# LSTM steps as 2x2 block products in Strassen's seven-product form, in a four-layer graph network

## The chip, the cores and the metric

The kernel runs on one core of a Trainium2 chip. Times are device microseconds of one execution, from its launch to its end, and the figure compared is the median of several. The core has five engines that work side by side and wait for each other through semaphores: TensorE (PE) multiplies matrices and writes to eight banks of accumulation memory (PSUM, 512 fp32 columns each), VectorE (DVE) and ScalarE (ACT) do element-wise work and read those banks, GpSimd (POOL) does element-wise work on the main on-chip memory (SBUF), and SyncE (SP) issues transfers. All data are fp32.

## The reference

The input x is (128, 64, 256): 128 graphs of 64 nodes with 256 features, and one 64x64 adjacency matrix. Each of four layers adds to x the result of a graph layer on `relu(layernorm(x))`:

```python
# layer 0: two graph convolutions, then four LSTMs over windows of p = 1..4 nodes
h = relu(adj @ (x @ Wg0 + bg0)); h = relu(adj @ (h @ Wg1 + bg1))
for p in range(1, 5):
    nw = 64 // p
    wins = h[:, :nw*p, :].reshape(B*nw, p, 256)
    # LSTM over the p nodes of a window; g = x_t @ Wih[p-1].T + h @ Whh[p-1].T + b
    # c = sigmoid(f)*c + sigmoid(i)*tanh(g);  h = sigmoid(o)*tanh(c)
    h = h.at[:, arange(nw)*p + p-1, :].set(last hidden state)
# layer 1: normalised adjacency, linear 256->512, batch norm, relu, linear 512->256, batch norm
# layer 2: three products with W[k], combined by diagonal, upper and lower part of adj
# layer 3: one attention head, qkv = x @ Wqkv, causal softmax(q k^T / 16 + adj) v, @ Wo
```

The first LSTM step of a window has no h term, as h starts at zero.

## The kernel before, in words

Rows are the 8192 nodes, in 16 pieces of 512 (`NS`) or 4 groups of 2048 (`NG`). Stages follow one another:

1. `graph_part` (lines 229 to 259): layer norm and the two graph convolutions, piece by piece, written to `hT`, which holds features in partitions (two halves `c`) and nodes along the free axis, one tile per group.
2. Lines 269 to 285: `wqkv` and `wo` are loaded and the products `wqk` and `wvo` of layer 3's weights are made (12 transposes and 8 products), before the LSTMs.
3. The LSTMs, for p = 1 to 4. The windows of a group are cut into blocks of at most 512 columns (16 windows of 32 graphs): N is 512 for p = 1, 2 and 4, and 320 or 352 for p = 3. `step` does one time step of one block: for each gate in the order i, g, f, o and each half of its 256 outputs, two products with `wih` and, from the second step on, two with `whh` into one bank (line 329), then one activation by ScalarE (line 331). VectorE makes the cell (338, 341 to 343), ScalarE its tanh (344), VectorE h (347) or the result in `hT` (351). Two blocks alternate, so that one's cell work lies beside the other's products. A scheduler orders the instructions there.
4. `first_product` (layer 1 up to its first linear layer, with `hs` copies by GpSimd at 395), batch norm 1, `second_product`, batch norm 2 (`bn_coeffs`).
5. `rest`: layers 2 and 3, piece by piece.

Within `pipelined` stages, as in any `manual_schedule` block, each engine's queue has its instructions in the order in which the code writes them. `psum` has eight one-bank buffers taken in turn by `bank()`. Pools on the left of SBUF (`hpool`, `lg`, `lh`, `pz`, `pb`, `wt`, `pc`) and on the right (`hlast`, `lw`, `first`, `late`) are stacked; a tile of a later pool waits for the last use of what lay in its place. The loads of `wih` and `whh` are issued by SP, most constants by ScalarE's queue.

Of the kernel before, what the change touches and what calls it, by code (L numbers as in the profile page):

```python
# [14 lines left out]
P = 128  # L15
# [5 lines left out]
def kernel(ctx: ExitStack, tc: tile.TileContext, a: dict, out: bass.AP):  # L21
# [40 lines left out]
    lstm_weights, lw = other_end("lw", 2)  # L62
# [22 lines left out]
    ones = const.tile([P, P], F32, tag="ones", name="ones")  # L85
# [4 lines left out]
    def block_diag(name, src):  # L90
        t = const.tile([P, P], F32, tag=name, name=name)
        nc.vector.memset(t, 0.0)
        for r in range(0, P, T):
            nc.scalar.dma_start(t[r : r + T, r : r + T], src)
        return t
# [9 lines left out]
    w1 = weight("w1", a["W1T"])  # L105
    w2 = weight("w2", a["W2T"])
    bn1 = load_const("bn1", a["bn1"], [P, 3, HC])
    bn2 = load_const("bn2", a["bn2"], [P, 3, KC])
    wqk = const.tile([P, KC, D], F32, tag="wqk", name="wqk")
    wvo = const.tile([P, KC, D], F32, tag="wvo", name="wvo")  # L110
# [79 lines left out]
    def to_token_major(src, add, dst):  # L190

        for q2 in range(0, Q, 2):
# [8 lines left out]
    hbuf = [(hpool if g < NG else hlast).tile([P, KC, GRP], F32, tag=f"hT{g}", name=f"hT{g}")  # L201
            for g in range(NG + 1)]
    hT = hbuf[1:]
# [63 lines left out]
    with tc.tile_pool(name="wt", bufs=1) as wt:  # L267
        wqkv = wt.tile([P, KC, 3 * D], F32, tag="wqkv", name="wqkv")
        nc.scalar.dma_start(wqkv, a["Wqkv"].rearrange("(c p) m -> p c m", p=P))
        wo = wt.tile([P, KC, D], F32, tag="wo", name="wo")  # L270
        nc.scalar.dma_start(wo, a["Wo"].rearrange("(c p) m -> p c m", p=P))
        wT = wt.tile([P, 3 * KC, D], F32, tag="wT", name="wT")
        for k in range(3):
            p_ = bank().rearrange("p (d c) -> p d c", d=KC)
            for d in range(KC):
                for c in range(KC):
                    nc.tensor.transpose(p_[:, d, ts(c, P)], wqkv[:, c, ts(k * KC + d, P)], ident)
            nc.vector.tensor_copy(wT[:, k * KC : (k + 1) * KC, :], p_)
        for left, right, to in ((0, wT[:, KC : 2 * KC, :], wqk), (2, wo, wvo)):
            p_ = bank().rearrange("p (c m) -> p c m", c=KC)  # L280
            for c in range(KC):
                for d in range(KC):
                    nc.tensor.matmul(p_[:, c, :], wT[:, left * KC + d, ts(c, P)], right[:, d, :],
                                     start=(d == 0), stop=(d == KC - 1))
            nc.vector.tensor_copy(to, p_)


    with tc.tile_pool(name="lg", bufs=2) as lg, \
            tc.tile_pool(name="lh", bufs=3) as lh:
        for p in range(1, NL + 1):  # L290
            l = p - 1
            wih = lw.tile([P, KC, G4], F32, tag="wih", name="wih")
            nc.sync.dma_start(wih, a["WihT"][l].rearrange("(c p) m -> p c m", p=P))
            whh = None
            if p > 1:
                whh = lw.tile([P, KC, G4], F32, tag="whh", name="whh")
                nc.sync.dma_start(whh, a["WhhT"][l].rearrange("(c p) m -> p c m", p=P))
# [4 lines left out]
            blocks = [(g, w0, w1 - w0) for g in range(NG) for w0, w1 in zip(cut, cut[1:])]  # L302
# [6 lines left out]
            def step(blk, j, state):  # L309
                last = j == p - 1  # L310
                N = blk[2] * GB
                gate = {}
                for name, gi, fn in (("i", 0, AF.Sigmoid), ("g", 2, AF.Tanh),
                                     ("f", 1, AF.Sigmoid), ("o", 3, AF.Sigmoid)):
                    if name == "f" and j == 0:
                        continue
# [39 lines left out]
            for k in range(0, len(blocks), 2):  # L356
                pair = [(blk, {}) for blk in blocks[k : k + 2]]
                for j in range(p):
                    for blk, state in pair:
                        step(blk, j, state)  # L360
# [228 lines left out]
```

## Time and profile before

| | us |
|---|---|
| median of three executions (2129.55 to 2130.78) | 2130.47 |
| the profiled execution | 2128.89 |
| its span, first to last instruction | 2127.2 |
| TensorE busy in the span | 2064.4 (97%) |
| VectorE, ScalarE, GpSimd busy | 788.5, 739.0, 139.0 |
| graph part: until the last matmul of line 252 | 0 to 189.0 |
| LSTMs: first to last matmul of line 329 | 202.4 to 1384.0 |
| first product and batch norm 1 | 1384 to 1569 |
| second product and batch norm 2 | 1569 to 1685 |
| rest | 1685 to 2127 |

Engines are busy side by side, so their sums pass the span. The ends of matmuls are modelled by the profiler, so a group's mean can be longer than the distance from one matmul to the next; that distance is read from the timeline. In the groups of instructions a row has line, engine and operation, the tiles written and read, shapes and count, then busy microseconds and mean nanoseconds of one, then the idle time of the engine ahead of them and who ended it.

### The profile page before, as it was taken

The page shows a single profiled execution, that of the slowest core. Times are in us where ns is not written, and L with a number is a line of the kernel's source. Part 1 is how long each engine was busy: PE and PEld are TensorE (multiplying, and loading weights), DVE is VectorE, ACT ScalarE, POOL GpSimd, SP SyncE. Part 2 cuts the span into 40 slices and gives each one's busy share as a digit, 9 for nine tenths or more (in the row PEclk, how much of TensorE's full clock was granted, in tenths as well). Part 3 has the DMA queues.
Part 4 walks back from the last instruction along what each step waited for, and adds up shares of the span by engine and source line. Part 5 has one row for each costly group of instructions (what it writes and reads, how often), then busy time and mean ns, then how long its engine had stood idle before and what let it go on. Part 6 is the DMA issues. An engine that isn't in the chain of part 4 may idle for free. (4 is left out here: it accounts for less than half of the span.)

```text
span 2127.2 us, 18649 instructions
## 1 busy us (share of the span) xinstructions
PE 2064.4 (97%) x7488; PEld 1241.0 (58%) x7488; DVE 788.5 (37%) x1569; ACT 739.0 (35%) x1267; POOL 139.0 (7%) x126
## 2 busy tenths in 40 slices
PE   6998999999999999999999999989999799999998
PEld 5775444444445666666444444455544478888887
DVE  5773222112121122121211211177744455555553
ACT  3553444332233233232322322234463033333332
POOL 1000000000000000000000000032200021111110
PEclk9999999999999999999999999999999899999999
DMA  5100000000001000000000000033300000111111
GB/s 193 50 30 20 0 0 20 0 0 0 0 0 40 1 0 1 0 1 0 0 0 0 0 0 0 0 121 97 107 10 0 30 20 20 41 40 41 44 47 40
DMA packets 35975, 54.26 MB, mean 26 GB/s; under 512 B 2608, under 2 KB 29488, under 8 KB 35888
## 3 DMA queue, kind: packets, MB, share of 16 engines
q1 hardware_dynamic: 31856, 49.29, 7.1%
q10 hardware_dynamic: 4032, 3.78, 0.6%
q8 instruction: 59, 0.97, 0.2%
q14 instruction: 28, 0.23, 0.0%
HBM read 36.28 MB, written 16.78 MB: 25 GB/s over the span
## 5 line engine op out<-in xcount | busy, mean ns | idle before, releaser
L329 PE MATMUL ps<-hT,wih 128*128 128x512 f32 (+2 forms) x2016 | 808.9, 541 | 0.0
L329 PEld LDWEIGHTS ps<-hT,wih 128*128 128x128 f32 x2016 | 383.0, 190 | 378.5 <-issue 313.3
L329 PE MATMUL ps<-hn,whh 128*128 128x512 f32 (+2 forms) x1152 | 466.3, 527 | 0.0
L329 PEld LDWEIGHTS ps<-hn,whh 128*128 128x128 f32 x1152 | 218.9, 190 | 200.4 <-issue 153.1
L176 ACT ACTIVATE ln_h<-x,ln_rn 128x256 f32<-128x256 f32 x192 | 99.6, 589 | 368.1 <-DVE ln_rn L173 363.2
L341 DVE TENSOR_TENSOR gi<-gi,gg 128x1024 f32<-128x1024 f32 (+2 forms) x36 | 38.2, 1062 | 385.6 <-ACT gg L331 385.6
L331 ACT ACTIVATE gi<-ps,lbias 128x512 f32<-128x512 f32 (+2 forms) x144 | 91.9, 638 | 235.0 <-PE ps L329 235.0
L331 ACT ACTIVATE gg<-ps,lbias 128x512 f32<-128x512 f32 (+2 forms) x144 | 91.9, 638 | 232.0 <-PE ps L329 232.0
L485 PE MATMUL ps<-wl,ag 128*128 128x256 f32 x768 | 169.6, 381 | 0.0
L485 PEld LDWEIGHTS ps<-wl,ag 128*128 128x128 f32 x768 | 145.7, 191 | 19.3
L331 ACT ACTIVATE go<-ps,lbias 128x512 f32<-128x512 f32 (+2 forms) x144 | 91.2, 634 | 89.2 <-PE ps L329 86.8
L338 DVE TENSOR_TENSOR cell<-gi,gg 128x1024 f32<-128x1024 f32 (+2 forms) x36 | 41.1, 1143 | 201.2 <-ACT gg L331 201.2
L395 POOL COPY hs<-hT 128x512 f32<-128x512 f32 x32 | 33.5, 1078 | 1228.9 <-PE ps L329 1228.9
L407 PE MATMUL ps<-ag,w 128*128 128x512 f32 x256 | 112.3, 592 | 0.0
L331 ACT ACTIVATE gf<-ps,lbias 128x512 f32<-128x512 f32 (+2 forms) x72 | 44.8, 622 | 164.9 <-PE ps L329 164.9
L342 DVE TENSOR_TENSOR cell<-gf,cell 128x1024 f32<-128x1024 f32 (+2 forms) x36 | 38.2, 1062 | 171.4 <-ACT gf L331 171.4
L172 POOL TENSOR_TENSOR ln_rn<-ln_rn,mhalf 128x4 f32<-128x4 f32 x64 | 64.6, 1010 | 537.1 <-DVE ln_rn L171 537.1
L344 ACT ACTIVATE gg<-cell 128x1024 f32<-128x1024 f32 (+1 forms) x72 | 68.7, 954 | 82.2 <-DVE cell L343 82.2
L351 DVE TENSOR_TENSOR hT<-go,gg 128x512 f32<-128x512 f32 (+2 forms) x72 | 47.1, 654 | 86.6 <-ACT go L331 62.4
L407 PEld LDWEIGHTS ps<-ag,w 128*128 128x128 f32 x256 | 47.5, 190 | 54.0 <-issue 50.7
L169 DVE BATCH_NORM_STATS2 ln_st<-x 128x6 f32<-128x256 f32 x192 | 76.9, 401 | 0.0
L347 DVE TENSOR_TENSOR hn<-go,gg 128x1024 f32<-128x1024 f32 (+2 forms) x36 | 38.2, 1062 | 94.9 <-ACT go L331 94.9
(127 smaller groups left out, 1965.7 us busy)
## 6 DMA issues: line engine op xcount, KB each, us to landing
xt<-in_x_dram SPq DMA_DIRECT2D x32, 512.0 KB, 4.5
x1d<-x SPq DMA_DIRECT2D x16, 512.0 KB, 2.9
x<-x1d SPq DMA_DIRECT2D x16, 512.0 KB, 4.6
out_dram<-x SPq DMA_DIRECT2D x16, 512.0 KB, 3.2
wih<-in_WihT_dram SPq DMA_DIRECT2D x4, 1024.0 KB, 6.2
whh<-in_WhhT_dram SPq DMA_DIRECT2D x3, 1024.0 KB, 7.8
wqkv<-in_Wqkv_dram ACTq DMA_DIRECT2D x1, 768.0 KB, 4.3
wl<-in_W_dram ACTq DMA_DIRECT2D x3, 256.0 KB, 3.1
```

The costliest lines, as they stand in the source:

```text
L169: nc.vector.bn_stats(st[:, q, :], src[:, q, :])
L172: nc.gpsimd.tensor_tensor(rn[:, 0, :], rn[:, 0, :], mhalf[:, :Q], ALU.pow)
L176: nc.scalar.activation(h[:, q, :], src[:, q, :], AF.Relu, bias=rn[:, 1, q : q + 1], scale=rn[:, 0, q : q + 1])
L329: nc.tensor.matmul(o_, w[:, c, ts(m, P)], r, start=(n == 0), stop=(n == len(ops) - 1))
L331: nc.scalar.activation(gt[:, hc, :N], p_[:, :N], fn, bias=lbias[:, l, m : m + 1])
L338: nc.vector.tensor_mul(c_, i_, g_)
L341: nc.vector.tensor_mul(i_, i_, g_)
L342: nc.vector.tensor_mul(c_, gate["f"][:, :, :N], c_)
L344: nc.scalar.activation(g_, c_, AF.Tanh)
L351: nc.vector.tensor_mul(cols(blk, c, j), gate["o"][:, c, :N].rearrange("p (w b) -> p w b", b=GB), gate["g"][:, c, :N].rearrange("p (w b) -> ...
L407: nc.tensor.matmul(p_, w1[:, c, ts(o, P)], ag[:, c, :], start=(c == 0), stop=(c == KC - 1))
L485: nc.tensor.matmul(p_[:, q, :], ag[:, c, k, ts(q2 + q, P)], wl2[k][:, c, :], start=(n == 0), stop=(n == 3 * KC - 1))
```

## The change

Two blocks of columns are now taken together as a 2x2 problem: the rows of the left factor are the two halves of a gate's 256 outputs, the inner blocks the two halves of the features, and the columns the two blocks of windows. From the second step on (`strassen`) each gate is made of seven block products in place of eight, each with one `wih` and one `whh` matmul. The factors are sums and differences: of weights, made by GpSimd (`weight_sums`) after each load; of the inputs, by VectorE (`input_sums`); of h, by VectorE after each step. The outputs are put together from three copies out of the accumulating bank by ScalarE and three additions by VectorE per gate, and four activations follow, three of them from SBUF. The first step of a window (`plain`) keeps its products. The cell's element-wise work moves from VectorE to GpSimd. Two gates are in work at a time (`staggered`), and the whole LSTM part is written in a `manual_schedule`.

The products of layer 3's weights move behind batch norm 2, with the copies by ScalarE in place of VectorE, and their loads ahead of `second_product`. `lw` has one buffer (with two for `wih`), `w1` and `w2` are loaded behind the LSTMs, the adjacency blocks and `ones` lie in `first`, and the spare group tile `hS` is made behind the LSTMs.

In the compiled program a stretch of the Strassen steps has, with A the older gate and B the younger, this order of products on TensorE: A7, B1, A4, B2, A3, B6, B5, then B7, C1, B4 and so on; the numbers are those of `product`. ScalarE's queue has the last activation of A, then what follows gate A (after f: the two tanhs of the cell), then B's third copy.

```diff
-    lstm_weights, lw = other_end("lw", 2)
+    lstm_weights, lw = other_end("lw", 1)
...
-    w1 = weight("w1", a["W1T"])
-    w2 = weight("w2", a["W2T"])
...
-    with tc.tile_pool(name="wt", bufs=1) as wt:
-        wqkv = wt.tile([P, KC, 3 * D], F32, tag="wqkv", name="wqkv")
...
+    A11, A12, A21, A22, S1, S2, S4, S3 = range(8)
+    def load_lstm(src, tag, bufs, sums):
+        n = 8 if tag == "wih" else 7
+        w = lw.tile([P, n, 4, P], F32, tag=tag, name=tag, bufs=bufs)
+        v = src.rearrange("(c p) (g h m) -> h c p g m", p=P, g=4, m=P)
+        for h in range(2):
+            for c in range(2):
+                nc.sync.dma_start(w[:, 2 * h + c], v[h, c])
+        return w
+    def weight_sums(w):
+        s3 = S3 if w.shape[1] == 8 else A21
+        g = nc.gpsimd
+        g.tensor_add(w[:, S1], w[:, A21], w[:, A22])
+        g.tensor_sub(w[:, S2], w[:, S1], w[:, A11])
+        g.tensor_sub(w[:, s3], w[:, A11], w[:, A21])
+        g.tensor_sub(w[:, S4], w[:, A12], w[:, S2])
+    def weight_of(w, k):
+        return (None, A11, A12, S4, A22, S1, S2, S3 if w.shape[1] == 8 else A21)[k]
+    GATES = (("i", 0, AF.Sigmoid), ("g", 2, AF.Tanh), ("f", 1, AF.Sigmoid), ("o", 3, AF.Sigmoid))
+    def staggered(jobs):
+        live = []
+        jobs = iter(jobs)
+        more = True
+        while live or more:
+            if more and (not live or (len(live) < 2 and live[-1][1] >= live[-1][2])):
+                job = next(jobs, None)
+                if job is None:
+                    more = False
+                else:
+                    live.append([job[0], 0, job[1], job[2]])
+            for x in list(live):
+                if next(x[0], "end") == "end":
+                    x[3]()
+                    live.remove(x)
+                else:
+                    x[1] += 1
+    with tc.tile_pool(name="lg", bufs=1) as lg, tc.tile_pool(name="lh", bufs=2) as lh, \
+            tc.manual_schedule():
+        wih = load_lstm(a["WihT"][0], "wih", 2, False)
         for p in range(1, NL + 1):
             l = p - 1
-            wih = lw.tile([P, KC, G4], F32, tag="wih", name="wih")
-            nc.sync.dma_start(wih, a["WihT"][l].rearrange("(c p) m -> p c m", p=P))
             whh = None
             if p > 1:
-                whh = lw.tile([P, KC, G4], F32, tag="whh", name="whh")
-                nc.sync.dma_start(whh, a["WhhT"][l].rearrange("(c p) m -> p c m", p=P))
+                whh = load_lstm(a["WhhT"][l], "whh", 1, True)
+                weight_sums(whh)
...
+            if nblk % 2 == 0 and (nw % nblk == 0):
+                pairs = [[(g, w0, w1 - w0) for w0, w1 in parts[k : k + 2]]
+                         for g in range(NG) for k in range(0, nblk, 2)]
+            else:
+                pairs = [[(g + d, w0, w1 - w0) for d in range(2)]
+                         for g in range(0, NG, 2) for w0, w1 in parts]
...
+            def input_sums(st, j):
+                N = st["N"]
+                t = lh.tile([P, 4, 512], F32, tag="tx", name="tx")
+                b = [[cols(blk, c, j) for c in range(KC)] for blk in st["blk"]]
+                t1, t2, t3, t4 = (wide(t[:, k, :N]) for k in range(4))
+                nc.vector.tensor_sub(t1, b[1][0], b[0][0])
+                nc.vector.tensor_sub(t2, b[1][1], t1)
+                nc.vector.tensor_sub(t3, b[1][1], b[1][0])
+                nc.vector.tensor_sub(t4, b[0][1], t2)
+                st["tx"] = t
...
+            def plain(st, j, gi, fn, G):
+                N = st["N"]
+                for n, blk in enumerate(st["blk"]):
                     for hc in range(KC):
+                        p_ = bank()
+                        for c in range(KC):
+                            nc.tensor.matmul(wide(p_[:, :N]), wih[:, 2 * hc + c, gi, :],
+                                             cols(blk, c, j), start=(c == 0), stop=(c == KC - 1))
                         m = gi * KC + hc
+                        nc.scalar.activation(G[:, n, hc, :N], p_[:, :N], fn,
                                              bias=lbias[:, l, m : m + 1])
+                        yield
...
+            def strassen(st, j, gi, fn, G):
+                N = st["N"]
+                b0, b1 = st["blk"]
+                tx, h, th = st["tx"], st["h"], st["th"]
+                t_in = [wide(tx[:, k, :N]) for k in range(4)]
+                x_of = (None, cols(b0, 0, j), cols(b0, 1, j), cols(b1, 1, j), t_in[3], t_in[0],
+                        t_in[1], t_in[2])
+                h_of = (None, h[:, 0, 0, :N], h[:, 0, 1, :N], h[:, 1, 1, :N], th[:, 2, :N],
+                        th[:, 0, :N], th[:, 1, :N], h[:, 1, 0, :N])
+                def product(p_, k, start=False):
+                    nc.tensor.matmul(wide(p_[:, :N]), wih[:, weight_of(wih, k), gi, :], x_of[k],
+                                     start=start, stop=False, skip_group_check=True)
+                    nc.tensor.matmul(p_[:, :N], whh[:, weight_of(whh, k), gi, :], h_of[k],
+                                     start=False, stop=True, skip_group_check=True)
+                def act(n, hc, src=None):
+                    m = gi * KC + hc
+                    to = G[:, n, hc, :N]
+                    nc.scalar.activation(to, to if src is None else src, fn,
+                                         bias=lbias[:, l, m : m + 1])
+                def add(n, hc, p_):
+                    to = G[:, n, hc, :N]
+                    nc.vector.tensor_add(to, to, p_[:, :N])
+                pa_ = bank()
+                product(pa_, 1, True)
+                nc.scalar.copy(G[:, 0, 0, :N], pa_[:, :N])
+                yield
+                pc_ = bank()
+                product(pc_, 2, True)
+                add(0, 0, pc_)
+                yield
+                product(pa_, 6)
+                nc.scalar.copy(G[:, 1, 0, :N], pa_[:, :N])
+                act(0, 0)
+                yield
+                pb_ = bank()
+                product(pb_, 5, True)
+                yield
+                product(pa_, 7)
+                nc.scalar.copy(G[:, 1, 1, :N], pa_[:, :N])
+                add(1, 1, pb_)
+                yield
+                product(pa_, 4)
+                act(0, 1, pa_[:, :N])
+                act(1, 1)
+                yield
+                product(pb_, 3)
+                add(1, 0, pb_)
+                yield
+                act(1, 0)
...
+                for i, (st, j) in enumerate(steps):
+                    last = j == p - 1
+                    N = st["N"]
+                    tiles, cut_ = {}, {}
+                    for name, gi, fn in GATES:
+                        G = lg.tile([P, 2, KC, 512], F32, tag=f"g{name}", name=f"g{name}")
+                        tiles[name], cut_[name] = G, G[:, :, :, :N]
+                        def post(name=name, i=i, st=st, j=j, g=cut_, last=last, N=N):
+                            if name == "i" and i + 1 < len(steps) and steps[i + 1][1] > 0:
+                                input_sums(*steps[i + 1])
+                            if name == "g" and j == 0:
+                                st["c"] = lh.tile([P, 2, KC, 512], F32, tag="cell", name="cell")
+                                c = st["c"][:, :, :, :N]
+                                each(nc.gpsimd.tensor_mul, c, g["i"], g["g"])
+                                each(lambda o_, i_: nc.scalar.activation(o_, i_, AF.Tanh), g["f"], c)
+                            elif name == "g":
+                                each(nc.gpsimd.tensor_mul, g["g"], g["i"], g["g"])
+                            elif name == "f":
+                                c = st["c"][:, :, :, :N]
+                                each(nc.gpsimd.tensor_mul, c, g["f"], c)
+                                each(nc.gpsimd.tensor_add, c, c, g["g"])
+                                each(lambda o_, i_: nc.scalar.activation(o_, i_, AF.Tanh), g["f"], c)
+                            elif name == "o" and last:
+                                for n, blk in enumerate(st["blk"]):
+                                    for c in range(KC):
+                                        nc.vector.tensor_mul(cols(blk, c, j), wide(g["o"][:, n, c]),
+                                                             wide(g["f"][:, n, c]))
+                            elif name == "o":
+                                h = lh.tile([P, 2, KC, 512], F32, tag="h", name="h")
+                                th = lh.tile([P, 3, 512], F32, tag="th", name="th")
+                                hN, tN = h[:, :, :, :N], th[:, :, :N]
+                                each(nc.vector.tensor_mul, hN, g["o"], g["f"])
+                                nc.vector.tensor_sub(tN[:, 0], hN[:, 1, 0], hN[:, 0, 0])
+                                nc.vector.tensor_sub(tN[:, 1], hN[:, 1, 1], tN[:, 0])
+                                nc.vector.tensor_sub(tN[:, 2], hN[:, 0, 1], tN[:, 1])
+                                nc.vector.tensor_sub(hN[:, 1, 0], hN[:, 1, 1], hN[:, 1, 0])
+                                st["h"], st["th"] = h, th
+                        if j == 0 and name == "f":
+                            continue
+                        if j == 0:
+                            yield plain(st, j, gi, fn, G), 3, post
+                        else:
+                            yield strassen(st, j, gi, fn, G), 4, post
+            if p < NL:
+                nxt = load_lstm(a["WihT"][p], "wih", 2, True)
+                weight_sums(nxt)
+            staggered(jobs())
+            if p < NL:
+                wih = nxt
...
+    spare = ctx.enter_context(tc.tile_pool(name="spare", bufs=1))
+    hbuf = [spare.tile([P, KC, GRP], F32, tag="hS", name="hS"), *hT]
+        w1 = weight("w1", a["W1T"], pz)
+        w2 = weight("w2", a["W2T"], pz)
...
+        wqk = late.tile([P, KC, D], F32, tag="wqk", name="wqk")
+        wvo = late.tile([P, KC, D], F32, tag="wvo", name="wvo")
+        products = ExitStack()
+        wt = products.enter_context(tc.tile_pool(name="wt", bufs=1))
+        wqkv = weight("wqkv", a["Wqkv"], wt)
+        wo = weight("wo", a["Wo"], wt)
...
+        with tc.manual_schedule():
+            wT = wt.tile([P, 3 * KC, D], F32, tag="wT", name="wT")
+            for k in range(3):
+                p_ = bank().rearrange("p (d c) -> p d c", d=KC)
+                for d in range(KC):
+                    for c in range(KC):
+                        nc.tensor.transpose(p_[:, d, ts(c, P)], wqkv[:, c, ts(k * KC + d, P)], ident)
+                nc.scalar.copy(wT[:, k * KC : (k + 1) * KC, :], p_)
...
+                nc.scalar.copy(to, p_)
+        products.close()
```

## The prediction

> **What bounds the kernel now.** First the page: busy shares and the PE row of the forty slices.
>
> ```profile
> PE 2064.4 (97%) x7488; PEld 1241.0 (58%) x7488; DVE 788.5 (37%) x1569; ACT 739.0 (35%) x1267; POOL 139.0 (7%) x126
> ...
> PE   6998999999999999999999999989999799999998
> ...
> POOL 1000000000000000000000000032200021111110
> ```
>
> TensorE is the bound and GpSimd (POOL) nearly unused. Then the groups of instructions by shape, for counts and durations.
>
> ```profile
> L329 PE MATMUL ps<-hT,wih 128*128 128x512 f32 x1312 | 589.1, 592 | 0.0
> ...
> L329 PE MATMUL ps<-hn,whh 128*128 128x512 f32 x640 | 300.7, 592 | 0.0
> ...
> L344 ACT ACTIVATE gg<-cell 128x1024 f32<-128x1024 f32 x48 | 50.4, 1051 | 52.2 <-DVE cell L343 52.2
> ...
> L461 POOL TENSOR_TENSOR x<-x,bl 128x1024 f32<-128x1024 f32 x16 | 37.6, 2352 | 38.2 <-ACT ln_h L176 35.7 <-issue 2.4
> ...
> L342 DVE TENSOR_TENSOR cell<-gf,cell 128x1024 f32<-128x1024 f32 x20 | 24.5, 1224 | 112.8 <-ACT gf L331 112.8
> ...
> L505 ACT COPY qk<-ps 128x512 f32<-128x512 f32 x32 | 16.8, 570 | 0.6 <-PE ps L503 0.6
> ```
>
> Each matmul of the code is two in the trace (the loops make 1008 `wih` products, the page has 2016). 592 ns is a modelled length; the pitch comes from the timeline, inside the LSTM and at its two neighbours:
>
> ```profile
> 601.08 0.69 ACT L331 ACTIVATE gg<-ps,lbias 128x512 f32<-128x512 f32 x1 [1.03 <-PE ps L329]
> ...
> 602.80 0.69 ACT L331 ACTIVATE go<-ps,lbias 128x512 f32<-128x512 f32 x1 [1.03 <-PE ps L329]
> ...
> 195.59 2.79 PE L277 MATMUL ps<-ident,wqkv 128*128 128x128 f32 x12 [6.46 <-DMA wqkv<-in_Wqkv_dram]
> ...
> 1569.07 3.43 PE L433 MATMUL ps<-hT,w 128*128 128x512 f32 x4 [4.86 <-ACT hT L425]
> 1572.34 1.88 PE L433 MATMUL ps<-z,w 128*128 128x512 f32 x4
> ```
>
> Two j=0 banks, two code matmuls (four in the trace) each, end 1.72 us apart: 0.429 us a trace matmul at N=512; the same reading gives 0.295 at 352 and 0.269 at 320. The LSTM runs from 202.4 to 1384.0, 1181.6 us; 1952 x 0.429 + 608 x 0.295 + 608 x 0.269 = 1180. It has no bubble: every matmul less is gained, every wait of TensorE lost in full. The last two lines show the cost of an idle gap: after 4.86 us, four matmuls take 3.3 us instead of 1.72. By the table of stretches the granted clock falls to 0.50 some 4.0 to 4.4 us after the last matmul (last at 189.0, 1564.2, 1680.6; drop at 193.0, 1568.6, 1684.7) and stays there 3.0 to 4.5 us into the next work.
>
> **What the Trainium skill says.** "TensorE: Matmul & The Clock Gate", What's actually happening: an idle window of about 3.4 us halves the clock, a busy one restores it; the trace agrees as above. The same page, Architectural detail: ScalarE, VectorE and GpSimd run their queues strictly in order; so an activation that waits holds all behind it. "GPSIMD Engine Reference", 3.1 Elementwise: a two-input add of 2048 fp32 takes 4497 ns, about twice VectorE's; the trace agrees (2352 against 1224 ns at 1024), and both points give 2.1 ns an element plus 0.2 us: estimates of 1.68 us at 704, 1.55 at 640, 1.28 at 512. Its 8. Key points has POOL and VectorE sharing their way to SBUF, in each other's way where VectorE reads two inputs from there; nothing in this trace shows it.
>
> **The change part by part.**
> *Matmuls.* Steps with j > 0 had 2304 trace matmuls (twice the 1152 of `whh`); seven products for eight leave 2016. Gone: 160 at 512, 64 at 352, 64 at 320: 68.6 + 18.9 + 17.2 = -104.7 us.
> *Weight products.* Last graph matmul done at 189.0, first LSTM matmul at 202.4. The gap (DMA of wqkv, 28 trace matmuls, copies, a 1.28 us table load) goes; the table load hides behind free banks: -13.4. Behind batch norm 2 TensorE stood still for 4.8 us (1680.6 to 1685.4), and the same 28 trace matmuls at full clock need about 5; the five ScalarE copies find it idle for 79.8 us. The first x1 load may wait for them: +1.
> *Loads of engines.* One Strassen step at N=512 takes TensorE 4 gates x 14 x 0.858 = 48 us. ScalarE: 4 x (3 copies of 0.57 + 4 activations of about 0.7) + 2 x 1.05 = 20; VectorE: 12 adds of 0.68, input sums 2.8, h and its sums 5.2 = 16; POOL 6 x 2.35 = 14. None is the bound by sum.
> *The wait that is new: the f gate.* In the compiled order of each Strassen step, ScalarE's queue has, behind the last f activation, the two cell tanhs, and right behind these the copy of bank `pa_` of the o gate that TensorE's product 4 waits for (it adds into that bank). The tanhs wait for POOL: f x c for both blocks, then both adds, in order. Time 0 is the end of the o gate's product 6, T one product (4 trace matmuls): 1.716 us at N=512. ScalarE starts 0.2 after the matmul slot (seen all over the LSTM): copy of o, activation of o, last activation of f, overlapping by some 0.1 each, f done at 2.0. POOL's first multiplication is long done; the second runs 2.1 to 4.4, the adds to 6.8 and 9.1; second tanh 9.1 to 10.15; copy to 10.6; product 4 starts at 10.7. In between TensorE has products 5, 7 and the next gate's 1: busy until 3T = 5.15. Stall 5.5 us. With the shorter rows at N=352: 7.9 - 3 x 1.18 = 4.4; at 320: 7.4 - 3 x 1.08 = 4.1. Strassen steps: p=2 four, p=4 six (N=512), p=3 four each at 352 and 320: 55 + 17.6 + 16.6 = +89. The last step of p=2, 3 and 4 has no next gate to fill with: + 1.7 + 1.2 + 1.7 = +4.6. VectorE queues nothing with two SBUF inputs in that stretch, so POOL is taken at its undisturbed 2.35.
> *Clock.* Ten stalls of 5.5 us exceed the 4.0 to 4.4 at which the clock falls: 1.9 us lost each (half of 3.8). Eight of 4.1 to 4.4 are on the edge, half counted: 19 + 7.6 = +27. Bounds 0 and 18 x 2.2 = 40.
> *Other waits.* In a plain step the tanh waits for one POOL product (2.35) while eight banks give TensorE slack: 0. At the start of p=3, whh (one buffer) loads after the last product of p=2, the next wih behind it: 7.8 us for 1 MB in the page, so some 12 for both, and POOL's eight weight sums (1.28 each) end near 18; its cell products, tanh and the o activations come after that, with eight banks full at about 18 to 19: +4. At p=2 and 4 the longer products (1.716) cover it. SP has nothing else queued there. The first wih sums stand in POOL's queue ahead of the third layer norm's pow: within 1 us. At the LSTM's end the hs copies now wait for add, activation and two multiplications behind the last matmul, about 3 us, of which the x load (landed 4 us after it) hides part: +2.5. w1 and w2 load there, 17 us ahead of their first use: 0.
> *Sum.* -104.7 - 13.4 + 89 + 4.6 + 27 + 4 + 2.5 + 1 = +10. On the profiled execution (2128.9, span 2127.2 plus 1.7) that is 2139; the median lies 1.6 higher: 2141.
>
> **Rivals.**
> *Cheaper stalls, faster.* If TensorE's clock stays up through the stalls: -118 + 94 + 7.5 = -17, 2113 us. Break-even is near: 118 less 7.5 over 18 stalls is 6.1 us each, cold clock included, against 6.7 above; three POOL operations are in each, so 0.2 us less in each decides. For it: POOL's row is one shape with a broadcast input. Against: skill and row lie on one line, and three gaps out of three cooled the clock.
> *A longer chain, slower.* The multiplications start only after all four f activations, or are slowed by VectorE at the shared memory interface: a fourth POOL operation, or as much, in each chain: 10 x 2.35 + 8 x 1.6 = +36, 2177. Against: the waits in the compiled order go by block.
> *The full gain.* If tanh and copy never collide, -118 + 8: 2021. It needs POOL's three operations to end within 3T, below 0.6 us each. Against: 2352 ns.
> *ScalarE or VectorE the bound:* excluded by 20 and 16 of 48 us.
>
> **How the numbers follow.** Even stalls 0.56, cheaper stalls 0.23, longer chain 0.16, full gain 0.05. The likeliest alone: 2125 to 2158 (clock bounds 0 to 40 against 27, stalls by a tenth). To hold 8 in 10 I reach over most of both neighbours: 2108 to 2178. A difference under 0.2% (4.3 us) can hardly be told from none. Of the likeliest case a tenth falls below, a fifth within, the rest above: faster 0.05 + 0.23 + 0.02, within 0.1, slower 0.6.
>
> **What would show it.** 2016 trace matmuls in the Strassen steps at an unchanged 0.429 pitch; the LSTM's start near 189; on POOL 36 multiplications and 36 adds of the f gate near 2.35 us at 1024; ScalarE's tanh waiting for POOL by some 7 us a step, TensorE waiting for the o gate's copy by 4 to 5.5 us in 18 places, and the clock row below 9 in p=2 and p=4. Wrong if TensorE waits elsewhere (product 7, bank reuse, VectorE's h sums), if POOL's operations take other than 2.35, or if the clock holds.

## The result, and the profile after

The changed kernel takes 2145.23 us (median; 2143.55 to 2146.85) against 2130.47 before: ratio 1.007, interval 1.0047 to 1.0093, so it is slower by 14.8 us. The prediction was 2141. Its profiled execution took 2143.55 us with a span of 2141.8, which is 14.6 more than before; the mean granted clock fell from 0.990 to 0.971.

First the page of the changed kernel: busy shares, then the rows of forty slices for TensorE, GpSimd and the granted clock, then the row of the groups whose idle time stands out.

```profile
PE 1998.2 (93%) x7200; PEld 1198.5 (56%) x7200; DVE 846.3 (40%) x1780; ACT 836.9 (39%) x1488; POOL 466.3 (22%) x294
...
PE   7999999999998989998999999889999899999998
...
POOL 2000214122224232223222222232200012111110
PEclk9999999999999999999999999989999999999999
...
L375 PE MATMUL ps<-tx,wih 128*128 128x512 f32 (+2 forms) x576 | 271.3, 554 | 89.8 <-ACT go L406 89.8
```

TensorE has 288 matmuls less (7200 for 7488), as the prediction counted, and its share falls from 97 to 93%: it waits. The last line says where: 89.8 us ahead of the matmuls of line 375 with an input sum `tx`, ended by ScalarE's copy of the o gate (L406). The clock row stays at 9 up to the slice in which the LSTMs end, although the loss there turns out to be 37 us: a tenth of a slice of 53 us is too coarse for it.

The table of waits (engine, line, what was waited for: total us, times, longest) has both links of the predicted chain:

```profile
ACT gf L449 <- POOL cell L420: 92.5, 36, 4.8
...
PE ps L375 <- ACT go L406: 89.8, 18, 7.1
```

ScalarE's tanh waits for GpSimd's cell state 36 times, and TensorE waits in 18 places for the copy that stands behind these tanhs. One of the 18, in p = 2, from the timeline of all engines (start, duration, instruction, in brackets the idle time before it and who ended it):

```profile
436.32 0.71 ACT L383 ACTIVATE gf<-gf,lbias 128x512 f32<-128x512 f32 x1
...
437.10 2.35 POOL L420 TENSOR_TENSOR cell<-gf,cell 128x1024 f32<-128x1024 f32 x1 [3.92 <-ACT gf L383]
...
439.30 1.02 PE L377 MATMUL ps<-h,whh 128*128 128x512 f32 x2
...
439.41 4.64 POOL L420 TENSOR_TENSOR cell<-cell,gg 128x1024 f32<-128x1024 f32 x2
441.78 1.06 ACT L449 ACTIVATE gf<-cell 128x1024 f32<-128x1024 f32 x1 [4.75 <-POOL cell L420]
444.08 1.06 ACT L449 ACTIVATE gf<-cell 128x1024 f32<-128x1024 f32 x1 [1.25 <-POOL cell L420]
445.05 0.57 ACT L406 COPY go<-ps 128x512 f32<-128x512 f32 x1
...
445.66 2.08 PE L375 MATMUL ps<-tx,wih 128*128 128x512 f32 x2 [5.34 <-ACT go L406]
```

The last f activation, three GpSimd operations of 2.35 us behind it, the second tanh, the copy, and then product 4, for which TensorE stood still for 5.34 us. And the first matmuls behind the wait take 2.08 us where the same two take 1.02 at full clock.

By stages, the LSTMs begin at 187.8 (before: 202.6 by the same reading) and last 1210.6 us (before 1181.4); from their end to the first transposes of `rest` it takes 304.0 us (301.5), and `rest` 439.4 (441.8): -14.8, +29.2, +2.5 and -2.4 make the span's +14.6.

### The profile page after: what moved, and what is told of

It is laid out like the page before. It is cut to its first block, busy times and chain, and to the rows that moved or that the text cites. A ratio compares the mean times of both kernels' runs of the same rounds, so it can differ in the third digit from the quotient of the medians.

```text
span 2141.8 us, 18882 instructions
## 1 busy us (share of the span) xinstructions
PE 1998.2 (93%) x7200; PEld 1198.5 (56%) x7200; DVE 846.3 (40%) x1780; ACT 836.9 (39%) x1488; POOL 466.3 (22%) x294
## 5 line engine op out<-in xcount | busy, mean ns | idle before, releaser
L375 PE MATMUL ps<-tx,wih 128*128 128x512 f32 (+2 forms) x576 | 271.3, 554 | 89.8 <-ACT go L406 89.8
L357 PE MATMUL ps<-hT,wih 128*128 128x512 f32 (+2 forms) x864 | 345.9, 562 | 2.6 <-ACT go L360 2.6
L357 PEld LDWEIGHTS ps<-hT,wih 128*128 128x128 f32 x864 | 165.1, 191 | 183.3 <-issue 158.0
L377 PE MATMUL ps<-h,whh 128*128 128x512 f32 (+2 forms) x576 | 260.6, 534 | 0.0
L375 PEld LDWEIGHTS ps<-tx,wih 128*128 128x128 f32 x576 | 111.0, 196 | 196.3 <-ACT go L406 102.4
L377 PE MATMUL ps<-th,whh 128*128 128x512 f32 (+2 forms) x432 | 203.8, 555 | 0.0
L375 PE MATMUL ps<-hT,wih 128*128 128x512 f32 (+2 forms) x432 | 201.0, 548 | 0.0
L420 POOL TENSOR_TENSOR gg<-gi,gg 128x1024 f32<-128x1024 f32 (+2 forms) x36 | 72.7, 2020 | 519.6 <-ACT gg L383 519.6
L377 PEld LDWEIGHTS ps<-h,whh 128*128 128x128 f32 x576 | 112.6, 195 | 104.5 <-issue 82.4
L420 POOL TENSOR_TENSOR cell<-gi,gg 128x1024 f32<-128x1024 f32 (+2 forms) x36 | 79.1, 2200 | 252.7 <-ACT gg L360 252.7
L375 PEld LDWEIGHTS ps<-hT,wih 128*128 128x128 f32 x432 | 86.6, 200 | 82.2 <-issue 58.9
L377 PEld LDWEIGHTS ps<-th,whh 128*128 128x128 f32 x432 | 86.5, 200 | 82.1 <-issue 65.3
```

The source lines that it names most:

```text
L357: nc.tensor.matmul(wide(p_[:, :N]), wih[:, 2 * hc + c, gi, :], cols(blk, c, j), start=(c == 0), stop=(c == KC - 1))
L375: nc.tensor.matmul(wide(p_[:, :N]), wih[:, weight_of(wih, k), gi, :], x_of[k], start=start, stop=False, skip_group_check=True)
L377: nc.tensor.matmul(p_[:, :N], whh[:, weight_of(whh, k), gi, :], h_of[k], start=False, stop=True, skip_group_check=True)
L420: fn(*(t[:, n] for t in tiles))
```

## The experiments

The theory to test had three parts: the waits come from the order of ScalarE's queue and not from work that is missing; their length is GpSimd's chain; and what the LSTMs lose beyond the waits is TensorE at half clock behind them. The rivals were a wait that only moves, another cause of the waits, and slower work in place of a slower clock. The experiments ran on three chips, on each of which the kernel before was measured again (medians of 2128.86, 2129.4 and 2129.84 us); each ratio is against the kernel before on its own chip.

### The tanhs later in the queue

```diff
-        live = []
+        live, later = [], []
...
-                    x[3]()
+                    act_later = x[3]()
+                    if act_later is not None:
+                        later.append([3, act_later])
                     live.remove(x)
                 else:
                     x[1] += 1
+            for y in list(later):
+                y[0] -= 1
+                if y[0] == 0 or not live:
+                    y[1]()
+                    later.remove(y)
...
-                                each(lambda o_, i_: nc.scalar.activation(o_, i_, AF.Tanh), g["f"], c)
+                                return lambda: each(
+                                    lambda o_, i_: nc.scalar.activation(o_, i_, AF.Tanh), g["f"], c)
```

> The changed kernel with one thing moved: the two tanhs of the cell state behind the f gate are put into ScalarE's queue three products later, behind the three copies of the o gate's banks instead of ahead of the third; POOL's chain itself is as slow as before. Theory (the waits are only a matter of queue order: the tanhs that wait for POOL stand ahead of the copy that TensorE needs): the waits for the copy, 89.8 us in 18 places, go, and with them the 37 us of cold clock: about 2145 - 92 - 37 = 2016, between 2008 and 2030, granted clock back at about 0.99. Rival (POOL's chain of 7 us is on the path in any order: the wait turns up at bank reuse, at the o activations or at the h sums that the next step's first recurrent product needs): above 2080. Result between: part of the wait has only moved.

Measured: 2016.5 us (2015.82 to 2018.38), ratio to the kernel before 0.9473 (0.9458 to 0.9487). What is left of the LSTMs' waits, by the table of TensorE's waits of this kernel:

```profile
PE ps L364 <- ACT go L367: 3.0, 1, 3.0
PE ps L382 <- ACT go L413: 1.9, 3, 0.7
```

And the same stretch of p = 2 in its timeline:

```profile
437.20 2.35 POOL L427 TENSOR_TENSOR cell<-gf,cell 128x1024 f32<-128x1024 f32 x1 [3.93 <-ACT gf L390]
...
438.74 0.59 ACT L413 COPY go<-ps 128x512 f32<-128x512 f32 x1 [1.62 <-PE ps L384]
...
439.50 4.67 POOL L427 TENSOR_TENSOR cell<-cell,gg 128x1024 f32<-128x1024 f32 x2
...
440.26 1.02 PE L382 MATMUL ps<-tx,wih 128*128 128x512 f32 x2
...
443.37 1.99 ACT L457 ACTIVATE gf<-cell 128x1024 f32<-128x1024 f32 x2
```

GpSimd runs the same three operations within 0.1 us of the times that they had before the edit. Only the copy no longer stands behind the tanhs: it goes at 438.74, TensorE goes on without a gap, and the tanhs run at 443.4, when nobody is held up. The granted clock is 1.00 over the whole LSTM stage of this run, which lasts 1082.5 us. So the chain's 7 us were never needed on TensorE's path; the queue put them there. This is also the best version of the study: 112 us faster than the kernel before, with the change's products as they are.

### The weight products alone

The kernel before with lines 269 to 285 moved behind batch norm 2:

```diff
-    with tc.tile_pool(name="wt", bufs=1) as wt:
-        wqkv = wt.tile([P, KC, 3 * D], F32, tag="wqkv", name="wqkv")
...
+        wqkv = weight("wqkv", a["Wqkv"], wt)
+        wo = weight("wo", a["Wo"], wt)
...
+        with tc.manual_schedule():
+            wT = wt.tile([P, 3 * KC, D], F32, tag="wT", name="wT")
...
+                nc.scalar.copy(wT[:, k * KC : (k + 1) * KC, :], p_)
```

> The kernel before with only the weight products of layer 3 moved behind the second batch norm, with their copies on ScalarE and their loads ahead of the second product; no Strassen steps. Theory (the gap of 13.4 us between graph and LSTM goes, and what is added behind the batch norm is hidden by its idle TensorE): 2116 to 2119. Rival (the gain is given back at the second batch norm or by the copies standing ahead of layer 3's loads): 2126 to 2131.

Measured: 2113.61 us (2112.56 to 2114.39) against 2128.86 of the same chip: -15.3, a little more than expected. The timeline of TensorE of this kernel shows the start of the LSTMs:

```profile
181.79 6.60 PE L252 MATMUL ps<-g,wg 128*128 128x512 f32 x15
188.23 18.19 PE L308 MATMUL ps<-hT,wih 128*128 128x512 f32 x42
```

They begin at 188.23, 14.4 us earlier than before, and last 1181.4 us as before. Nothing is given back at batch norm 2; the span is 16.0 us shorter, so some 1.6 us come from there. The granted clock offers a reason: behind batch norm 2 the kernel before is at half speed in 1684.66 to 1698.31 and 1715.38 to 1722.20, 20.5 us; this one for 10.2 us, in 1677.31 to 1684.14 and 1701.20 to 1704.62, and so is the changed kernel (1708.27 to 1715.10, 1732.16 to 1735.58). The products keep TensorE busy where it stood still.

Between this kernel and the one with later tanhs lie the seven products and little else: LSTM stages of 1181.4 and 1082.5 - 4.9 of waits = 1077.6 us. The 288 matmuls are worth 103.8 us.

### GpSimd's order by block

```diff
-                                each(nc.gpsimd.tensor_mul, c, g["f"], c)
-                                each(nc.gpsimd.tensor_add, c, c, g["g"])
+                                for n in range(2):
+                                    nc.gpsimd.tensor_mul(c[:, n], g["f"][:, n], c[:, n])
+                                    nc.gpsimd.tensor_add(c[:, n], c[:, n], g["g"][:, n])
```

> The changed kernel with POOL's four operations of the f gate reordered: multiply and add of block 0, then multiply and add of block 1, so that behind the last f activation POOL has two operations to do instead of three (the first multiply and add are done by then). Theory (the length of the stall is POOL's chain, an operation at a time): each stall is shorter by one POOL operation, 2.35 us at 1024, 1.68 and 1.55 at the shorter rows: 5.3 -> 3.0, 4.2 -> 2.5, 3.8 -> 2.2 us, 43 us less in 20 places; and stalls of 3 us hardly cool the clock, 30 to 37 us less: 2065 to 2076. If the clock cools as before: about 2102. Rival (the copy waits for something else than POOL's chain, such as VectorE): no change, 2145.

Measured: 2105.88 us (2104.82 to 2114.84), ratio 0.990 (0.988 to 0.9921). The table of waits of this kernel:

```profile
ACT gf L450 <- POOL cell L449: 61.2, 18, 3.9
...
PE ps L375 <- ACT go L406: 56.6, 18, 4.9
```

The stalls are shorter by about one operation, 5.34 to 3.17 us at N=512, 4.22 to 2.72 and 3.76 to 2.40 at the shorter rows: the length is GpSimd's chain. But the second half of the expectation fell. Waits of 2.4 to 3.2 us (3.8 to 4.9 at the ends of the stages) cooled the clock in 15 of 18 places, among them 12 of the 15 that are not ends, and the time is near the 2102 of "as before". In the table of stretches (span of the stretch, then busy time and number of instructions for PE, PEld, DVE, ACT and POOL, the granted clock, DMA share, GB/s), two of them of this kernel, with a wait of 3.17 us in the first:

```profile
440.93:444.34 3.41, 0.35 (x1) 0.00 (x0) 0.00 (x0) 1.47 (x3) 1.91 (x1) 1.00 0.00 0
444.34:447.75 3.41, 3.30 (x4) 1.50 (x5) 0.69 (x1) 0.54 (x2) 0.00 (x0) 0.50 0.00 0
```

TensorE idles in nearly all of the first stretch at full clock, and the half clock comes with the second, in which it works for 3.30 of the 3.41 us. So the price of this wait lies almost wholly behind it, in the next 3.41 us.

### Keeping TensorE busy in the stalls

```diff
+                if gi == 3:
+                    keep = bank()
+                    for _ in range(3 if N == 512 else 4):
+                        nc.tensor.matmul(keep[:, :N], whh[:, A22, gi, :], h_of[1],
+                                         start=True, stop=True, skip_group_check=True)
                 product(pa_, 4)
```

> The changed kernel with work added: 3 matmuls of 512 columns (4 where the rows are shorter), whose result nothing reads, stand just ahead of the o gate's product 4 in all 18 Strassen steps with a stall, so that TensorE is busy for 2.6 us (2.4 and 2.2) of each stall and idle for less than 3 us at a time. Clock theory (the stalls cost 37 us more than their length, as half-speed work behind them): the clock stays up, the stalls end when they did, about 2145 - 37 = 2108, between 2100 and 2118, with 54 to 60 more code matmuls than before. Rival (what is above the sum of the stalls isn't the clock but slower work elsewhere): 2145 or more, since the added matmuls are then at best free.

Measured: 2124.64 us (2121.83 to 2127.05), ratio 0.998. Adding 62 matmuls made the changed kernel some 20 us faster (19 with each kernel taken against the kernel before on its own chip), which excludes the rival; but the gain is only a little over half of the clock theory's 37. In this kernel 7 of the 18 stalls still cooled the clock, all of them at N=512, where 2.78 us (4.5 at the ends of p = 2 and 4) stay idle, and the wait at the start of p = 3. None of the eight at the shorter rows did (1.6 to 1.9 us idle, 2.9 at the end of p = 3).

The starts and ends of the half-clocked stretches, read in slices of half a microsecond, gave the rule. In the changed kernel all 21 of them behind 400 us, from 445.34 to 1735.58, begin and end at 1.61 or 1.62 us more than a multiple of 3.4133 us, and each lasts one, two, three or four such periods; in the runs of this section the same holds with another offset in each (1.53 here). So the clock is set anew every 3.413 us on a grid that runs through the execution without regard to the work, from how busy TensorE was in the period before. At full clock, every period in which TensorE was busy for 1.37 us or less was followed by one at half clock. At half clock, within the LSTM stages, it stayed so after periods with up to 2.83 us of work and came back after 2.85 or more; behind batch norm 2, 2.82 us in the changed kernel and 2.78 in the moved-alone run were enough.

For the prediction's drop "4.0 to 4.4 us after the last matmul" this means that three gaps of the kernel before had similar positions on their grid. Two stalls of the changed kernel of the same length, 3.76 and 3.77 us at N=320, differ only in that position. The stretches of both, first the period with the wait and then the next:

```profile
721.81:725.23 3.42, 1.36 (x5) 1.04 (x6) 0.49 (x1) 1.61 (x4) 0.93 (x1) 1.00 0.01 2
725.23:728.64 3.41, 3.41 (x7) 2.04 (x7) 0.52 (x1) 0.97 (x2) 0.00 (x0) 0.50 0.00 0
899.31:902.73 3.42, 1.51 (x6) 1.09 (x7) 0.49 (x1) 1.58 (x5) 0.78 (x1) 1.00 0.00 0
902.73:906.14 3.41, 3.41 (x13) 2.25 (x12) 1.75 (x3) 0.94 (x3) 0.00 (x0) 1.00 0.00 0
```

1.36 us of work in the first period: half clock from 725.23, when TensorE had been back at work since 723.87. 1.51 us: full clock, and 13 matmuls in the next period where the other got 7.

### More filling

Two kernels put the rule to the test. The count is 4 and 6 in the first, 5 and 7 in the second:

```diff
+                if gi == 3:
+                    keep = bank()
+                    for _ in range(6 if st.get("end") else 4):
+                        nc.tensor.matmul(keep[:, :N], whh[:, A22, gi, :], h_of[1],
+                                         start=True, stop=True, skip_group_check=True)
...
+                        st["end"] = i + 1 == len(steps)
                         if j == 0:
```

> The changed kernel with more added work than before: 4 matmuls whose result nothing reads, ahead of the o gate's product 4 in each Strassen step, 6 in the last step of a stage, so that TensorE idles 1.9 us (1.9 and 1.6 at the shorter rows) in one go. Theory formed from the earlier traces: the granted clock is set anew every 3.413 us, on a grid that runs through the whole execution; a period in which TensorE is busy for less than about 1.4 us (41%) is followed by one at half speed, and a period at half speed is left only if TensorE is busy in it for more than about 2.85 us. So no wait below 2.0 us can cool the clock wherever it falls on the grid: no cold period at the 18 stalls (7 stalls had one or two with 3 matmuls, where 2.8 us stayed idle), and the 37 us of lost speed of the changed kernel come back: about 2108, between 2104 and 2112. Rival (the clock falls by the total length of a stall, or its loss isn't what separates the times): no better than with 3 matmuls, 2120 to 2127.

Measured: 2117.67 us (2115.24 to 2119.39): between the two expectations. 4 of the 18 stalls still cooled the clock, all of them waits of 1.91 to 1.93 us at N=512, so the threshold had been put too low. Two such waits of this kernel, each with the period behind it:

```profile
443.12:446.53 3.41, 1.49 (x5) 0.41 (x3) 0.04 (x1) 2.16 (x4) 1.77 (x1) 1.00 0.00 0
446.53:449.94 3.41, 3.41 (x8) 1.60 (x9) 0.65 (x1) 1.71 (x3) 0.00 (x0) 1.00 0.00 0
497.73:501.14 3.41, 1.49 (x4) 0.49 (x3) 0.69 (x1) 2.12 (x3) 0.85 (x1) 1.00 0.00 0
501.14:504.55 3.41, 3.41 (x5) 1.35 (x4) 0.00 (x0) 1.30 (x2) 0.00 (x0) 0.50 0.00 0
```

Both have 1.49 us of work, and only one is followed by half clock: a wait of 1.92 us that lies within one period is on the threshold. Over the LSTM stages of all these runs the boundary lies between 1.40 us (the least that kept the full clock) and 1.51 (the most that lost it), with the ends of matmuls modelled; just behind the LSTMs, 1.56 and 1.64 us lost it too.

> The changed kernel with 5 added matmuls (7 in the last step of a stage), whose result nothing reads, ahead of the o gate's product 4, so that 1.1 us (1.3 and 1.1 at the shorter rows) of each stall stay idle. With 4 of them, 1.9 us stayed idle and 4 of the 10 waits of 1.9 us still cooled the clock, those that lay within one period of the grid. Theory: a wait of 1.1 us leaves every period busy for at least 2 us, so none of the 18 stalls cools the clock; the stalls end where they did, and LSTM stage and time fall by all of the 37 us: about 2108, between 2104 and 2112 (one period at the start of the third stage may still be cold). Rival (something else than the clock, such as TensorE's restart, costs time behind each stall): about as with 4 matmuls, 2115 to 2120, without cold periods.

Measured: 2108.43 us (2106.82 to 2109.89), ratio to the kernel before 0.990. None of the 18 stalls cooled the clock, nor did the start of p = 3, and the time is the 2108 of the theory. The LSTM stage as one stretch, first of the changed kernel and then of this one (mean granted clock 0.96 and 1.00, the third figure from the end), and the remaining wait for the copy from the table of waits of this kernel:

```profile
187.80:1398.40 1210.60, 1118.13 (x2881) 561.55 (x2879) 296.95 (x464) 478.12 (x794) 321.32 (x164) 0.96 0.01 4
```

```profile
187.90:1362.20 1174.30, 1151.83 (x3073) 581.92 (x3071) 296.90 (x464) 478.13 (x794) 321.57 (x164) 1.00 0.02 4
```

```profile
PE ps L375 <- ACT go L406: 19.9, 18, 1.3
```

96 matmuls whose results nothing reads, set into waits that were there, give back 36.8 us (36.2 with each kernel taken against the kernel before on its own chip). That is the direct price of the half clock in the changed kernel.

### The cell on VectorE

```diff
-                                each(nc.gpsimd.tensor_mul, c, g["f"], c)
-                                each(nc.gpsimd.tensor_add, c, c, g["g"])
+                                each(nc.vector.tensor_mul, c, g["f"], c)
+                                each(nc.vector.tensor_add, c, c, g["g"])
```

> The changed kernel with the f gate's two multiplications and two adds on VectorE instead of POOL, in the same order and with the tanhs where they were. Theory (the stall is three operations long, whatever engine runs them): 1.224, 0.892 and 0.826 us an operation (VectorE's rows of the kernel before) for 2.349, 1.672 and 1.538: 3.4, 2.3 and 2.1 us less in each, so stalls of 2.0, 1.9 and 1.6 us and 3.7, 3.0 and 3.7 at the ends of the stages, 52 us less in all; by the grid only the ends can cool the clock, at most 6 periods of 3.4 us, so 27 to 37 us of speed come back: about 2060, between 2054 and 2068. Rival (VectorE, which also has the o gate's adds and the sums of h and x, becomes the wait): stalls as long as before, 2110 or more.

Measured: 2068.53 us (2068.14 to 2070.19), ratio 0.9713 (0.9697 to 0.973). In the table of waits:

```profile
ACT gf L449 <- DVE cell L420: 38.9, 18, 2.5
PE ps L375 <- ACT go L406: 37.3, 18, 3.9
```

52.5 us of waits less, as worked out, at 1.91, 1.81 and 1.56 us each. The upper edge of the expected range is passed by half a microsecond since 4 of the waits of 1.91 us also fell within one period and cooled the clock, beside the three ends and the start of p = 3: 13.4 us lost where 0 to 10 were expected. VectorE's further work didn't make it the wait.

### All runs on one line

If waits and half clock are the whole story, each LSTM stage less its waits, its added matmuls and half of the half-clocked time in which TensorE had work must leave the same number. The added matmuls count with the pitches of the prediction (two trace matmuls of 0.429, 0.295 or 0.269 us each).

| kernel | LSTM stage | waits (copy, start of p = 3) | added work | lost to half clock | left |
|---|---|---|---|---|---|
| changed | 1210.6 | 92.4 | 0 | 37.0 | 1081.2 |
| 3 matmuls added | 1189.1 | 48.8 | 43.8 | 15.0 | 1081.5 |
| 4 matmuls added | 1183.2 | 36.0 | 57.0 | 8.5 | 1081.7 |
| 5 matmuls added | 1174.3 | 22.5 | 70.1 | 0 | 1081.7 |
| GpSimd by block | 1171.0 | 59.1 | 0 | 30.6 | 1081.3 |
| cell on VectorE | 1134.4 | 39.5 | 0 | 13.4 | 1081.5 |
| tanhs later | 1082.5 | 4.9 | 0 | 0 | 1077.6 |

Six agree within 0.5 us. The seventh lies 3.6 to 4.1 lower, of which 2.9 is a matter of reading: a matmul's modelled end lies 0.16 us behind its slot (1.02 us for two against a pitch of 0.86), so each of 18 waits is shown 0.16 too short. About 1 us stays unexplained.

## Why the prediction was right

The direction and the time were right (2141 for 2145.23, inside the likeliest case's own range), and so was the mechanism of the case named likeliest. How close the sum came is in part luck: the clock was put 10.0 us too low, and the start of the LSTMs, the start of p = 3 and `rest` together 6.2 too high. The chances don't add up as stated: a tenth of the likeliest case's 0.56 is 0.056 and not 0.02, which makes it 0.34 for faster, 0.11 for within and 0.55 for slower. The steps, by what the profiled executions and the runs show:

| step | predicted | measured | from |
|---|---|---|---|
| matmuls of seven products | -104.7 | -103.8 | LSTM stages of the moved-alone and the later-tanhs runs |
| weight products, start of the LSTMs | -13.4 | -14.8 | 202.6 to 187.8 |
| waits of the f gate, with the ends of p = 2, 3, 4 | +93.6 | +92.7 | 89.8 shown, and 18 x 0.16 |
| half clock | +27 | +37.0 | half-clocked time behind the waits; 36.8 by the filled run |
| start of p = 3 | +4 | +2.6 | wait at line 357 |
| end of the LSTMs to `rest` (measured with the moved products, which stand there) | +2.5 | +2.5 | 301.5 to 304.0 |
| `rest` (predicted: its first load waits for the moved products) | +1 | -2.4 | 441.8 to 439.4 |
| sum | +10 | +13.8 | span +14.6 |

**The wait.** Chain, place and length held. At N=512 the stall of 5.5 us is 5.34 with the 0.16 of the slot: 5.50. At 352 it is 4.38 for 4.4, at 320 3.92 for 4.1. GpSimd's durations that no row had shown came out as the estimates: 1672 and 1538 ns for 1.68 and 1.55 us. VectorE and ScalarE were never the bound, as counted. Moving the tanhs and shortening the chain changed the waits as the theory said. Two of the signs came otherwise than stated: the clock row did not show p = 2 and p = 4 below 9, and ScalarE's tanh waits for GpSimd by 5.1 us a step on average (92.5 us in 18 steps, 6.0 in the step shown) in place of some 7.

**The clock is the mis-sized term.** The step that failed is the sentence that the clock falls 4.0 to 4.4 us after the last matmul, with the eight shorter stalls "on the edge, half counted". It measured 37.0 us in place of 27, inside the bounds of 0 to 40. The third of its own gaps did not fit its "3.0 to 4.5 us into the next work" either: there the half clock lasted from 1684.66 to 1698.31, through 6.67 us of work and a second wait of 6.23 us. There is no fixed delay after the last matmul. In its place there is the grid: a period of 3.413 us with less than about 1.4 to 1.5 us of work is followed by one at half clock, and another follows unless TensorE works for some 2.8 us of it. 17 of the 18 stalls were followed by work at half clock, the shorter ones too, on average by 4.35 us of it. The Trainium skill had the core of this, in a sentence of the section that the prediction cites ("TensorE: Matmul & The Clock Gate", What's actually happening): the window is 3413 ns long and runs free of the kernel. The prediction used the window's length and passed over the second half. The traces agree with that sentence to 0.01 us. With the page's section Why this matters for your kernels, which advises against idle gaps of more than about 3 us, they do not: gaps shown with 1.91 to 1.93 us sufficed in 8 places of two runs here, and the measurement decides.

**The moved products.** The start gained 1.4 us more than the 13.4, and `rest` gained 2.4 where +1 was expected. The run that moves them alone shows a gain of the same kind, 15.3 us in all. Of the +2.5 up to `rest`, 0.4 is theirs (301.5 to 301.9 in that run). The step that failed is the +1, for a first load that may wait behind the five copies: it priced what is added and not that TensorE, kept busy there, goes into `rest` with 10.2 us at half clock in place of 20.5. That this is the cause is a reading of the clock in three kernels; it wasn't tested by itself.

**The rivals.** "Cheaper stalls, faster" asked for a clock that stays up through the waits. The run with 5 matmuls added comes closest to that case, and it gave 2108 where the prediction worked out 2113: the break-even was as near as said. "A longer chain" is excluded by the timeline, which has three GpSimd operations behind the last f activation. "The full gain" needed tanh and copy not to collide; it was priced at 2021 and ruled out because GpSimd is too slow for it. Its price was right, since the run with later tanhs takes 2016.5, but GpSimd's speed isn't what it needs: the order of one queue is enough.

## What to carry to other kernels

On an engine that takes its queue in order, an instruction that waits for a long chain should stand behind the short ones that another engine needs now; here two tanhs ahead of one copy cost 128 us of 2145 (waits and half clock), and with the same work three products later 1.9 us of waits are left for the copies of the o gate. Price a gap of TensorE not by its length against a threshold but by the periods of 3.4 us that it leaves mostly empty: each is followed by a period at half clock, paid by the matmuls behind the wait. A mean busy share, or a clock row of forty slices, doesn't show this; the table of stretches at the grid of the clock does.

## What was not expected of the hardware

The half clock can come after the restart: in the stall at 723.87 TensorE had worked for 1.4 us at full clock when it fell. In the changed kernel this is so in 3 of the 17 stalls that cooled the clock, and in four runs with shorter waits (3 and 4 matmuls added, GpSimd by block, cell on VectorE) in 23 of 33. And the clock depends on where the waits fall on the grid, whose offset differed from run to run (1.61, 0.60, 1.53, 2.80, 3.16 us and so on), so the number of half-clocked periods is partly a matter of luck.

Beside GpSimd, VectorE was slower in one place, which the prediction had not priced. At the start of p = 3, the timeline of all engines of the changed kernel:

```profile
685.91 3.92 POOL L420 TENSOR_TENSOR cell<-gi,gg 128x704 f32<-128x704 f32 x2 [4.76 <-ACT gg L360]
685.93 0.48 DVE L345 TENSOR_TENSOR tx<-hT,hT 128x320 f32<-128x320 f32 x1
686.44 1.85 DVE L346 TENSOR_TENSOR tx<-hT,tx 128x320 f32<-128x320 f32 x1
688.22 1.96 DVE L347 TENSOR_TENSOR tx<-hT 128x320 f32<-128x320 f32 x1
690.10 0.48 DVE L348 TENSOR_TENSOR tx<-hT,tx 128x320 f32<-128x320 f32 x1
```

Two of VectorE's differences with both inputs in SBUF take 1.85 and 1.96 us beside GpSimd's two multiplications; the 13 differences of this shape with no GpSimd operation beside them take 0.48 to 0.49. GpSimd's pair takes 3.92 us where two of 1.67 would take 3.34. The first of the four, which starts with the pair, still takes 0.48. The same two are as slow at the same place in the run with later tanhs (1.85 and 1.96 us); that the two engines hold each other up is read from this, and no run tests it. Here nobody waits for it. A plan that sends work from VectorE to GpSimd in order to run both at once should look for it.
